# A row LSTM over a 128 x 128 image: the products of input channels 0-63 as three 64-row products per pixel pair, in pairs, with one PSUM ring and a written order

## The chip, the cores and the metric

One core of a Trainium2 chip. The metric is device time of one execution in microseconds (us); lower is better. Times are medians over the runs of one job unless a profile is named. A profile is of one execution.

Words used: a **half-step** is one image row for one half of the batch (4 of 8 images); there are 128 rows and two halves, so 256 half-steps. A **gate tile** is 128 of the 384 gate channels; there are three, A, B and C. A **unit** is one fp32 product with 128 rows of weights and 256 columns; by the records it is two **passes**. A **change of row tiling** is a switch of TensorE between products of 128 rows and products of 64 rows, which can lie two at a time in the array. In the lines of the profile, PE is TensorE's products, PEld its weight loads, DVE VectorE, ACT ScalarE, POOL GpSimd.

## The reference, cut to what matters

```python
# x: (8, 96, 128, 128) fp32; normalised over 32 groups of channels, then
its = conv(gn(x), W_is * mask, 1 x 3)            # taps: left neighbour and (masked) centre
def step(carry, row_in):                          # over the 128 rows
    h, c = carry
    gates = conv(h, W_ss, 3) + row_in             # taps: left, centre, right along the row
    f, i, o = sigmoid(...), sigmoid(...), sigmoid(...)
    g = tanh(...)
    c = f * c + i * g
    h = o * tanh(c)
    return (h, c), h
out = x + h of all rows
```

The rows depend on each other through h; the two batch halves do not, so the kernel alternates them.

## The kernel before

Pixels are held as even and odd ones. With the sum vs = e + o and the difference vf = o - e of neighbours, two products of 256 columns give the three-tap convolution's common part (m1 + m2 for even pixels, m1 - m2 for odd ones), and two more on the shifted differences vd finish it. The contraction has 128 rows: 96 channels of h, and below them channels 64 to 95 of x. Channels 0 to 63 of x cannot fit there. They have a tile xn of their own, 64 channels shifted by a pixel above the same 64 channels unshifted, and one 512-column product of 128 rows.

```python
    def normalise_own(engine, s, k, j, lo, hi):
        norm(engine, xn[s][k % 2][:, lo:hi, :, j, :],
             xr[s][:, j, lo * W : hi * W].rearrange("p (r j t) -> p r t j", r=hi - lo, t=2), 0, 1, s * BH + j)
    ...
        def both(self, a):
            self.mm(a, 0, 1, self.vs, start=True)
            self.mm(a, 1, 2, self.vf)
        def copy(self, a):
            ...
            nc.scalar.activation(
                self.m1[a], self.ps[a][:, 0:HB], AF.Identity, bias=bias[:, a : a + 1]
            )
        def sums(self, a):
            lo, hi = self.ps[a][:, 0:HB], self.ps[a][:, HB : 2 * HB]
            nc.vector.tensor_add(lo, self.m1[a], hi)
            nc.vector.tensor_sub(hi, self.m1[a], hi)
        def rest(self, a):
            xi = xn[self.s][self.row // R % 2][:, self.row % R]
            self.mm(a, None, 4, xi.rearrange("p t b j -> p (t b j)"))
            self.mm(a, 0, 0, self.vd[:, 1])
            self.mm(a, 1, 3, self.vd[:, 0], stop=True)
    ...
    for row in range(NT):
        for s in range(NH):
            ...
            now.both(a0); prev.tanh(a2); prev.gated(); now.copy(a0); now.sums(a0)    # joined here
            ...
            now.rest(a0); now.tanh(a0); now.sigmoid(a0)
            ...
```

PSUM has a pool of two banks for each gate tile, and two banks for the statistics.

## Time and profile before

| | before |
|---|---|
| median | 2143.21 us (2142.21 to 2143.75, 3 runs) |
| head, up to half-step 1 | 142 us, loads and group statistics |
| recurrence, 255 half-steps | 1990 us |
| TensorE busy in the recurrence | all of it |
| granted clock | 0.997 |

The busy line says how long each engine had work; the chain says what set the end. The two differ for an engine that is busy and not late. Here the same engine leads in both, and the lines that show it stand in the prediction below. Two lines are added from the waits of the kernel before; the columns are who waited for whom, then us in total, times, longest us:

```profile
POOL vd L327 <- DVE vf L326: 753.9, 202, 19.9
ACT g L380 <- PE ps L354: 469.5, 767, 2.1
```

GpSimd (POOL) waited 754 us for work. It has room. ScalarE waited for the products, as everyone does behind the engine that sets the pace.

### The profile page before, as it was taken

What the parts mean: (1) busy time and instruction counts of PE and PEld (TensorE: products, weight loads), DVE (VectorE), ACT (ScalarE), POOL (GpSimd) and SP (SyncE); (2) the same over time, 40 slices, a digit from 0 to 9 for tenths busy, and PEclk for the clock granted to TensorE, in tenths of its full rate; (3) what the DMA queues carried; (4) which work ended last, traced back from release to release, by engine and by line L of the source; (5) the groups of instructions that cost most, each with busy time, mean ns of one, the idle gap of its engine ahead of it and who ended that gap; (6) DMA issues with size and microseconds to landing.
All of it is one profiled execution on the core that took longest, in us unless ns stands there. A gap on an engine that the chain in (4) does not pass through costs nothing.

```text
span 2140.7 us, 24553 instructions
## 1 busy us (share of the span) xinstructions
PE 2014.5 (94%) x7738; PEld 1451.8 (68%) x7738; DVE 1571.4 (73%) x3268; ACT 1387.0 (65%) x2611; POOL 1037.4 (48%) x1365
## 2 busy tenths in 40 slices
PE   0079999999999999999999999999999999999998
PEld 0057777777777777777777777777777777777776
DVE  6887777777777777777777777777777777777776
ACT  2446666666666666666666666666666666666666
POOL 1126555555555554555555555555555555555542
PEclk9999999999999999999999999999999999999999
DMA  9984234444323444432344443234444323444411
GB/s 395 421 249 94 76 81 109 108 109 95 75 76 80 109 108 109 97 72 77 80 109 109 109 101 71 76 79 109 108 109 93 80 75 79 109 109 109 100 38 30
DMA packets 104303, 236.46 MB, mean 110 GB/s; under 512 B 6000, under 2 KB 10352, under 8 KB 98288
## 3 DMA queue, kind: packets, MB, share of 16 engines
q1 hardware_dynamic: 104176, 234.91, 42.9%
q8 instruction: 62, 1.02, 0.2%
q14 instruction: 65, 0.53, 0.1%
HBM read 184.55 MB, written 50.33 MB: 110 GB/s over the span
## 4 chain that ended last, share of the span: by engine, by line
PE 93%; DMA 4%; DVE 2%; ACT 0%; SPq 0%; issue 0%; POOL 0%; POOLq 0%; ACTq 0%
PE ps L354 93%; DMA piece<-in_x_dram 3%; DVE bst L528 2%; DMA xn<-in_x_dram 1%; PE spin L153 0%; ACT piece L184 0%; ACT piece L187 0%; SPq L517 0%; DVE st L534 0%; PE pv L221 0%; DVE ps L371 0%; ACT L184 0%; PE dm L221 0%; DVE ps L370 0%; DVE hx L409 0%
## 5 line engine op out<-in xcount | busy, mean ns | idle before, releaser
L354 PEld LDWEIGHTS ps<-vd,wl 128*128 128x128 f32 x3072 | 583.7, 190 | 407.1 <-issue 366.7
L354 PE MATMUL ps<-xn,wl 128*128 128x512 f32 x1536 | 795.6, 599 | 0.6 <-DVE ps L371 0.6
L354 PE MATMUL ps<-vd,wl 128*128 128x256 f32 x3072 | 788.4, 379 | 0.0
L380 ACT ACTIVATE g<-ps 32x512 f32<-32x512 f32 x768 | 453.5, 590 | 469.5 <-PE ps L354 469.5
L327 POOL TENSOR_TENSOR vd<-hx 128x512 f32<-128x512 f32 x256 | 266.0, 1039 | 946.5 <-DVE vf L326 753.9
L364 ACT ACTIVATE m<-ps,wl 128x256 f32<-128x256 f32 x768 | 358.2, 466 | 181.8 <-PE ps L354 181.8
L354 PE MATMUL ps<-vs,wm 128*128 128x256 f32 x1536 | 457.8, 380 | 0.0
L354 PE MATMUL ps<-vf,wm 128*128 128x256 f32 x1536 | 457.1, 379 | 0.0
L384 ACT ACTIVATE ps<-ps 96x512 f32<-96x512 f32 x768 | 442.9, 577 | 16.2
L388 DVE TENSOR_TENSOR ps<-ps,c 96x512 f32<-96x512 f32 x256 | 178.0, 695 | 372.7 <-ACT ps L384 372.7
L371 DVE TENSOR_TENSOR ps<-m,ps 128x256 f32<-128x256 f32 x768 | 329.2, 429 | 26.3
L370 DVE TENSOR_TENSOR ps<-m,ps 128x256 f32<-128x256 f32 x768 | 324.5, 422 | 16.9 <-ACT m L364 1.4
L416 POOL TENSOR_TENSOR x<-x,hx 96x512 f32<-96x512 f32 x254 | 328.4, 1293 | 0.0
L354 PEld LDWEIGHTS ps<-xn,wl 128*128 128x128 f32 x1536 | 270.5, 189 | 74.5 <-DVE ps L371 32.4
L354 PEld LDWEIGHTS ps<-vs,wm 128*128 128x128 f32 x1536 | 292.2, 190 | 40.1 <-DVE vs L325 0.2
L354 PEld LDWEIGHTS ps<-vf,wm 128*128 128x128 f32 x1536 | 292.3, 190 | 39.9
L391 DVE TENSOR_TENSOR g<-ps,g 96x512 f32<-96x512 f32 x256 | 175.9, 687 | 106.8 <-ACT g L380 106.8
L279 POOL TENSOR_SCALAR hx<-x,rstd,nmr 32x512 f32<-32x512 f32 (+2 forms) x256 | 206.2, 805 | 25.4
L279 POOL TENSOR_SCALAR xn<-xr,rstd,nmr 128x512 f32<-128x512 f32 (+2 forms) x256 | 207.2, 809 | 0.2
L409 DVE TENSOR_TENSOR hx<-ps,th 96x512 f32<-96x512 f32 x256 | 173.8, 679 | 0.7 <-ACT th L399 0.7
L395 DVE TENSOR_TENSOR c<-ps,g 96x512 f32<-96x512 f32 x256 | 173.8, 679 | 0.0
L399 ACT ACTIVATE th<-c 96x512 f32<-96x512 f32 x256 | 158.0, 617 | 2.1 <-DVE c L395 2.1
(80 smaller groups left out, 448.5 us busy)
## 6 DMA issues: line engine op xcount, KB each, us to landing
xr<-in_x_dram SPq DMA_DIRECT2D x124, 512.0 KB, 9.2
x<-in_x_dram SPq DMA_DIRECT2D x62, 768.0 KB, 8.9
out_dram<-x SPq DMA_DIRECT2D x62, 768.0 KB, 5.3
piece<-in_x_dram SPq DMA_DIRECT2D x16, 1024.0 KB, 11.7
x<-in_x_dram SPq DMA_DIRECT2D x62, 256.0 KB, 6.2
xs<-in_x_dram SPq DMA_DIRECT2D x15, 1024.0 KB, 12.3
xn<-in_x_dram SPq DMA_DIRECT2D x15, 1024.0 KB, 12.5
out_dram<-x SPq DMA_DIRECT2D x2, 576.0 KB, 3.7
```

The lines of the kernel that those rows point to most:

```text
L279: engine.tensor_scalar(dst, src, scale, shift, ALU.mult, ALU.add)
L327: diff = nc.gpsimd.tensor_sub(vd.rearrange("p t (b j) -> p t b j", b=BH), strided(h[:, 0, 0, :], 1, [(BH * JP - 1, 2), (JP, BH), (1, J)]), ...
L354: nc.tensor.matmul(o, wt[p][:, bass.ts(a, P)], rhs, start=start, stop=stop, skip_group_check=True)
L364: nc.scalar.activation(self.m1[a], self.ps[a][:, 0:HB], AF.Identity, bias=bias[:, a : a + 1])
L370: nc.vector.tensor_add(lo, self.m1[a], hi)
L371: nc.vector.tensor_sub(hi, self.m1[a], hi)
L380: nc.scalar.activation(self.g[a * 32 : (a + 1) * 32], self.ps[a][C:P], AF.Tanh)
L384: nc.scalar.activation(gate, gate, AF.Sigmoid)
L388: nc.vector.tensor_mul(f, f, cs[self.s].rearrange("p t b j -> p (t b j)"))
L391: nc.vector.tensor_mul(self.g, self.ps[1][0:C], self.g)
L395: nc.vector.tensor_add(c, self.ps[0][0:C], self.g)
L416: (nc.gpsimd if row + 1 < NT else nc.vector).tensor_add(xo, xo, h)
```

## The change

The intent is to give TensorE fewer columns. Channels 0 to 63 get the same sum-and-difference treatment as h: P on the sum of a pixel pair, Q on the difference e - o, and E on the difference between the previous odd pixel and this one. Each has 64 rows and 256 columns. The data and the weights are stored twice, in rows 0-63 and in rows 64-127, and gate tile A uses the low half, B the high one and C one or the other by batch half, so that two products can lie side by side in the array. Nine products of 64 rows in 4.5 pairs should cost 4.5 units where the three 512-column products cost six. In return GpSimd makes the pair sums and differences, one of three bias copies moves to VectorE, all PSUM tiles share one ring of eight banks, and one written order covers two half-steps, with P and Q issued a half-step ahead.

```diff
-        tc.tile_pool(name="ps", bufs=2, space=bass.MemoryType.PSUM)
+        tc.tile_pool(name="ps", bufs=8, space=bass.MemoryType.PSUM)
...
+    def combine(xw, n, total, differences):
+        e, o = xw[:, 0:n, 0:J], xw[:, 0:n, J + 1 :]
+        nc.gpsimd.tensor_add(total, e, o)
+        nc.gpsimd.tensor_sub(
+            differences,
+            strided(xw[:, 0, :], 0, [(W + 1, n), (J, 2), (1, J)]),
+            strided(xw[:, 0, :], J + 1, [(W + 1, n), (0, 2), (1, J)]),
+        )
+    def own_image(s, k, j):
+        to = xs[s][k % 2]
+        widen(nc.gpsimd, xw[0], 0, R, s, j, 0)
+        combine(xw[0], R, to[:, :, 0, j, :], to[:, :, 1:3, j, :])
...
+        def own(self, a, i):
+            low = a == order["A"] or (a == order["C"] and self.s == 0)
+            rhs = self.xs[:, i].rearrange("p b j -> p (b j)")
+            self.mm(a, i % 2, wo[i], rhs, slice(0, C2) if low else slice(C2, P))
...
         def copy(self, a):
...
+            if a == order["A"] and self.row + self.s > 0:
+                nc.vector.tensor_scalar(self.m1[a], m1, column, None, ALU.add)
+            else:
+                nc.scalar.activation(self.m1[a], m1, AF.Identity, bias=column)
...
-            self.mm(a, None, 4, xi.rearrange("p t b j -> p (t b j)"))
...
+    PERIOD = (
+        "2A 1A siB' fg' 2B taB' cpA 1B loA 3C' cpB hiA 0C' loB 1C taC' hiB 2C siC' 0A gt'",
+        "3A cpC ce' 0B loC th' hiC", "X", "ou' F' S' D' re'", "3B taA siA",
+    )
+    PRODUCTS = (
+        "P+A P+B Q+A Q+B P+C P*A Q+C EA EB EC",
+        "Q+A P+B P+C Q+B Q+C EB EA EC",
+    )
```

In the written order, a mark `'` is the half-step before, `+` the next one, `*` the one after that; 1, 2, 0, 3 are the products on vs, vf and the two of vd; "X" is replaced by the two lines of PRODUCTS in turn.

## The prediction

> **What bounds the kernel now.** I read the page from the top: busy shares, slices, the chain that ended last, then the groups, and last two stretches of the timeline. First the busy shares, the PE slices and the chain (part 1, part 2 and part 4 of the page of the kernel before):
>
> ```profile
> PE 2014.5 (94%) x7738; PEld 1451.8 (68%) x7738; DVE 1571.4 (73%) x3268; ACT 1387.0 (65%) x2611; POOL 1037.4 (48%) x1365
> PE   0079999999999999999999999999999999999998
> ...
> PE 93%; DMA 4%; DVE 2%; ACT 0%; SPq 0%; issue 0%; POOL 0%; POOLq 0%; ACTq 0%
> ```
>
> TensorE has work from the third slice to the end and 93% of the chain is its products. A busy PE need not be a fast PE, so I looked at the pitch. The chain in order of time has a single piece for the whole recurrence:
>
> ```profile
> 142.83 1990.10 PE ps L354 x7650
> ```
>
> That is 255 half-steps (128 rows, two batch halves, the first one done in the head): 1990.1 / 255 = 7.80 us each, and 7650 / 255 = 30 records, so each of the 15 fp32 products of a half-step is two passes. The timeline of TensorE alone, one half-step:
>
> ```profile
> 2109.39 0.59 PE L354 MATMUL ps<-vs,wm 128*128 128x256 f32 x2
> 2109.82 0.59 PE L354 MATMUL ps<-vf,wm 128*128 128x256 f32 x2
> ...
> 2111.98 1.05 PE L354 MATMUL ps<-xn,wl 128*128 128x512 f32 x2
> 2112.87 1.03 PE L354 MATMUL ps<-vd,wl 128*128 128x256 f32 x4
> ```
>
> A 256-column product starts 0.43 us after the one before it (2109.39 to 2109.82), the 512-column one takes twice that (0.89, 0.86 elsewhere), the two vd products 0.86 together. In units of 256 columns a half-step has 3 x (1 + 1 + 2 + 2) = 18, and 7.80 / 18 = 0.433 us a unit. The array is full, at a granted clock of 0.997; only fewer columns, or columns side by side, make this shorter. The head (142.8 us, mostly input loads) and the tail (some 7 us) are fixed costs.
>
> **What the Trainium skill says.**
> - "TensorEngine Tiling (Array Packing)", Key Properties: tiles run independently and in parallel, and changing the tiling mode drains the engine. Its gotcha on PSUM pressure says that row tiles must not be in one bank at once; the change sends the members of a pair to different banks. The kernel before has only 128-row products, so its trace shows none of this.
> - "TensorE: Matmul & The Clock Gate", LDWEIGHTS and Part 3: a weight load costs by its columns, not its rows, and products start and end in program order. The trace before agrees on order. On the loads it has a usable number: the 4-column products of the statistics, which are nearly all load.
>
> ```profile
> 135.68 0.36 PE L221 MATMUL dm<-st,wl 128*128 128x4 f32 x2 [4.28 <-DVE st L534]
> 135.90 0.59 PE L221 MATMUL pv<-st,wl 128*128 128x4 f32 x4
> ```
>
>   Two passes in 0.22 us: 0.11 us a load, although the record of one says 0.190 in the groups. Today a pass of 0.215 hides one load easily.
> - "SBUF — State Buffer", Who interferes with whom: a VectorE instruction with two SBUF inputs and a GpSimd instruction that reads SBUF block each other. The trace before is arranged to avoid it: GpSimd's vd waits for VectorE's vf for 753.9 us in all, and vs and vf take 428 and 418 ns.
>
> **The change part by part.** The groups that I price from:
>
> ```profile
> L384 ACT ACTIVATE ps<-ps 96x512 f32<-96x512 f32 x768 | 442.9, 577 | 16.2
> L388 DVE TENSOR_TENSOR ps<-ps,c 96x512 f32<-96x512 f32 x256 | 178.0, 695 | 372.7 <-ACT ps L384 372.7
> L371 DVE TENSOR_TENSOR ps<-m,ps 128x256 f32<-128x256 f32 x768 | 329.2, 429 | 26.3
> L416 POOL TENSOR_TENSOR x<-x,hx 96x512 f32<-96x512 f32 x254 | 328.4, 1293 | 0.0
> L327 POOL TENSOR_TENSOR vd<-hx 128x512 f32<-128x512 f32 x256 | 266.0, 1039 | 946.5 <-DVE vf L326 753.9
> ```
>
> *TensorE.* Removed: three 512-column 128-row products, 6 units, 2.60 us. Kept: 12 units, 5.20 us. Added: nine 64-row products of 256 columns (P, Q, E for three gate tiles). Alone each would still cost a unit; in pairs on the two row halves they cost 4.5 units = 1.95 us, so at best 7.15 us a half-step, 0.65 less. Three things stand against the 1.95. (1) Loads: a pair has four passes, so four loads; 4 x 0.11 = 0.44 against 0.433, about 2.00 for 4.5 pairs. (2) An fp32 product is two passes in program order, so the low product's second pass can run beside the high product's first: full rate inside a run, but one extra pass, 0.217, at the end of each of the run (one run per half-step). (3) Two mode changes per half-step. Two passes that start 0.215 apart end 0.59 after the first start, so a pass lives 0.375, 0.16 beyond its stream; if a drain exposes all of it, 2 x 0.16 = 0.32. Sum if all of it shows: 5.20 + 2.00 + 0.22 + 0.32 = 7.74 us. I take the middle of 7.15 and 7.74, because nothing in this trace says how much of (2) and (3) the hardware hides: **7.44 us**, 0.36 less than now.
>
> *VectorE.* One of three bias copies moves to it from ScalarE (about 0.43, estimated from the 128x256 row). Work: sums 3 x (0.429 + 0.422) = 2.55, the four 96x512 steps 0.695 + 0.687 + 0.679 + 0.679 = 2.74, vs and vf 0.85, copy 0.43: 6.57 us, up from 6.14. Fits in 7.44, but little is left.
>
> *ScalarE.* 2 copies x 0.466 + 3 x 0.590 + 3 x 0.577 + 0.617 = 5.05 us, down from 5.52. Not a bound.
>
> *GpSimd.* vd 1.04, residual 1.29, two normalisations 0.81 each as now (3.95), plus the pixel-pair sum (about 0.52, half of the 128x512 row) and the two differences (1.04): 5.5 us. It fits, but in the old order GpSimd was idle whenever vf and vs ran; now it ends only about 1 us before them.
>
> *PSUM and order.* The eight banks in one ring let the x products of the next half-step (P, Q) run before h is there, so they fill what would be a wait for h. By the written order C's last product ends 2.75 us into a half-step, then tanh 0.6, gated 0.7, cell 0.7, tanh 0.6, output 0.7, vf 0.4: about 6.5 to 7.0, just ahead of the next half-step. The recurrence is off the path, with slack of half a microsecond or less.
>
> *Head.* More weights, GpSimd pair work for the first rows in one lump: I allow +5 us. So 2143 + 5 - 255 x 0.36 = 2056, given as **2055 us**.
>
> **The rivals.**
> - *No overlap of row tiles* (or loads that serialize with the 0.190 us of their records): 9 units instead of 4.5, or 4 x 0.19 = 0.76 a pair. Then 5.20 + 3.4 to 3.9 = 8.6 to 9.1 us, 2350 to 2470 us. For it: nothing here has shown two products side by side. Against it: the 0.11 pitch of the loads, the skill's page, and a schedule written around pairs that would make no sense otherwise. I give it 5%.
> - *VectorE becomes the bound.* Loop: the first tile's vs product starts, siB ends some 0.4 later, then fg, copy and all the rest, 6.57 with a few waits, until vs of the next half-step: about 7.15 to 7.25 with handovers. That is a floor of about 2000 us even where TensorE pairs ideally; it would show as PE waiting for vs or vf.
> - *GpSimd collides with vf and vs.* Where a block has two shared normalisations in one half-step, GpSimd needs 6.3 us and its last instruction can still run when vf wants to start; a wait of up to 0.8 in a quarter of the half-steps, some 50 us at worst, partly absorbed.
> - *Drains eat the gain*: all of (1) to (3) exposed, 7.74 us and 2130 to 2140 us, the same time as now.
>
> **Range and chances.** Ideal pairs with VectorE's floor give 1995; all costs exposed give 2133. So 1990 to 2130 for 8 in 10. Faster by over 2% needs under 2100, a half-step under 7.61. The estimate sits 0.17 below that, and the drains must be nearly fully exposed to miss it: 0.75. Within 2%: 0.16, the exposed drains or a collision. Slower: 0.09, no overlap or a new wait of VectorE and GpSimd.
>
> **What the profile after would show.** Right: pairs of 64-row products starting close together at 0.43 to 0.45 us a pair, a gap of 0.1 to 0.2 us at each entry and exit of their run, PE still over 90% of the chain, half-step near 7.4, VectorE at 88%, GpSimd near 72%. Wrong: a pair at 0.76 or more (loads or no overlap); PE idle with vf, vs or a sum as releaser (VectorE or GpSimd bound); vs and vf well above 0.43 us (collision); a head longer by much more than 5 us; or gaps at the mode changes larger than 0.16.

## The result, and the profile after

The changed kernel took 2087.9 us (2086.93 to 2088.49, 4 runs) beside 2143.48 us for the kernel before on the same chip: a ratio of 0.9741, interval 0.9724 to 0.9758. A ratio is the mean time of one kernel's runs over that of the other's of the same rounds, so it is not quite the ratio of the medians. It is faster by 2.6%, inside the range, with a gain of 56 us where 88 were forecast.

The busy shares and the chain by engine, of the page of the changed kernel:

```profile
PE 1949.5 (93%) x10810; PEld 1586.3 (76%) x10810; DVE 1704.4 (82%) x3522; ACT 1322.2 (63%) x2352; POOL 1449.1 (69%) x1636
...
PE 91%; DMA 3%; POOL 2%; DVE 2%; ACT 1%; issue 0%; SPq 0%; POOLq 0%
```

TensorE still leads both. GpSimd rose from 48% to 69% and is new in the chain, with 2%. The chain in order of time says where that 2% lies (start us, us, what; the view shows the longest pieces alone, and these are the last five of them up to the long one):

```profile
204.75 7.64 PE ps L376 x40
213.35 1.04 POOL vd L476
214.40 1.25 POOL x L493
217.15 1.03 POOL xs L312
218.22 1855.35 PE ps L376 x10360
```

From 218 us to 2074 us the chain is TensorE alone: 10360 passes of 42 a half-step are 246.7 half-steps in 1855.35 us, 7.52 us each (7.80 before). Before that, GpSimd's work is threaded through the chain. These are two different stories, so the traces were compared at fixed marks, the starts of VectorE's vf of a half-step:

| mark | before | after | after minus before |
|---|---|---|---|
| vf of half-step 1 | 142.11 | 146.25 | +4.1 |
| vf of half-step 11 | 218.89 | 234.32 | +15.4 |
| vf of half-step 255 | 2122.79 | 2069.40 | -53.4 |
| end | 2140.7 | 2086.6 | -54.1 |
| mean half-step, 20 to 240 | 7.803 | 7.521 | -0.282 |

The steady part gains 244 x 0.282 = 68.8 us. The head and the first ten half-steps lose 15.4, where the steady pace would have given 2.8 in those ten. The rest of this section is the steady part: TensorE's timeline over one run of 64-row products.

```profile
999.43 0.59 PE L376 MATMUL ps<-vd,wl 128*128 128x256 f32 x2
999.95 1.57 PE L376 MATMUL ps<-xs,wx 64*128 64x256 f32 x12
1001.35 0.38 PE L376 MATMUL ps<-xs,wl 64*128 64x256 f32 x1
1001.36 0.38 PE L376 MATMUL ps<-xs,wx 64*128 64x256 f32 x1
1001.57 0.38 PE L376 MATMUL ps<-xs,wl 64*128 64x256 f32 x1
1001.58 0.38 PE L376 MATMUL ps<-xs,wx 64*128 64x256 f32 x1
1001.78 0.60 PE L376 MATMUL ps<-xs,wl 64*128 64x256 f32 x4
1002.31 0.70 PE L376 MATMUL ps<-vd,wl 128*128 128x256 f32 x2
```

The records at 1001.35 and 1001.36 are passes of two products, one on each row half; the next two follow 0.22 us later. The pairs run wholly side by side. Ten products, 20 passes, fill 999.95 to 1002.31, 2.36 us; 5 x 0.432 would be 2.16. The missing 0.2 is one half of what the two ends of the run cost; the other half falls on the 128-row passes beside it. Single records, over 225 runs between 300 and 2000 us, have these medians: a steady step between passes is 0.216; the last 128-row pass to the first 64-row pass is 0.309, and that one to the next of its row half 0.320; at the exit 0.306 and 0.320. So an entry costs 0.093 + 0.104 and an exit 0.090 + 0.104, **0.39 us a half-step**. The first pass behind each change is itself longer (0.70 for two records at 1002.31, 0.59 elsewhere). Then 16.5 units x 0.432 + 0.39 = 7.52, the measured half-step; the formula has nothing left over.

The groups that answer to those of before (line, engine, operation, out<-in, shapes, count | busy us, mean ns | idle before, releaser):

```profile
L476 POOL TENSOR_TENSOR vd<-hx 128x512 f32<-128x512 f32 x256 | 266.4, 1041 | 464.9 <-DVE vs L466 461.9
L376 PE MATMUL ps<-xs,wx 64*128 64x256 f32 x3072 | 457.7, 394 | 3.1 <-POOL xs L311 2.5
...
L376 PEld LDWEIGHTS ps<-xs,wx 64*128 64x128 f32 x3072 | 322.7, 187 | 112.1 <-issue 84.2
L436 DVE TENSOR_TENSOR ps<-ps,c 96x512 f32<-96x512 f32 x256 | 178.0, 695 | 267.5 <-ACT ps L432 267.5
...
L493 POOL TENSOR_TENSOR x<-x,hx 96x512 f32<-96x512 f32 x254 | 329.6, 1298 | 0.0
...
L312 POOL TENSOR_TENSOR xs<-xw 128x512 f32<-128x512 f32 x256 | 274.1, 1071 | 0.0
```

A weight load of 64 rows has a record as long as one of 128 (187 against 190 ns), yet two of them fit under one pass of 0.216. VectorE's idle time ahead of its forget step fell from 373 to 268 us, GpSimd's ahead of vd from 947 to 465: both are fuller, neither is late once the recurrence runs.

### The profile page after: what moved, and what is told of

Its sections match the earlier page's. It is cut to its first block, busy times and chain, and to the rows that moved or that the text cites. A ratio compares the mean times of both kernels' runs of the same rounds, so it can differ in the third digit from the quotient of the medians.

```text
span 2086.6 us, 31236 instructions
## 1 busy us (share of the span) xinstructions
PE 1949.5 (93%) x10810; PEld 1586.3 (76%) x10810; DVE 1704.4 (82%) x3522; ACT 1322.2 (63%) x2352; POOL 1449.1 (69%) x1636
## 4 chain that ended last, share of the span: by engine, by line
PE 91%; DMA 3%; POOL 2%; DVE 2%; ACT 1%; issue 0%; SPq 0%; POOLq 0%
PE ps L376 90%; DMA piece<-in_x_dram 2%; DVE bst L669 1%; DMA wl<-in_w_dram 1%; DMA xs<-in_x_dram 1%; PE spin L167 0%; POOL xw L295 0%; POOL hx L295 0%; POOL xs L312 0%; POOL vd L476 0%; POOL x L493 0%; ACT piece L200 0%; ACT piece L203 0%; SPq L658 0%; POOL xs L311 0%
## 5 line engine op out<-in xcount | busy, mean ns | idle before, releaser
L376 PE MATMUL ps<-vd,wl 128*128 128x256 f32 x3072 | 816.5, 388 | 5.0 <-POOL vd L476 4.3
L376 PE MATMUL ps<-xs,wx 64*128 64x256 f32 x3072 | 457.7, 394 | 3.1 <-POOL xs L311 2.5
L432 ACT ACTIVATE ps<-ps 96x512 f32<-96x512 f32 x768 | 418.8, 572 | 16.4 <-PE ps L376 0.2
L376 PEld LDWEIGHTS ps<-xs,wx 64*128 64x128 f32 x3072 | 322.7, 187 | 112.1 <-issue 84.2
L418 ACT ACTIVATE m<-ps,wl 128x256 f32<-128x256 f32 x513 | 243.5, 475 | 89.1 <-PE ps L376 75.4
L312 POOL TENSOR_TENSOR xs<-xw 128x512 f32<-128x512 f32 x256 | 274.1, 1071 | 0.0
L376 PE MATMUL ps<-xs,wl 64*128 64x256 f32 x1536 | 264.7, 376 | 1.5 <-DVE ps L425 1.3
L295 POOL TENSOR_SCALAR hx<-x,rstd,nmr 32x512 f32<-32x512 f32 (+1 forms) x260 | 206.6, 794 | 26.7
L295 POOL TENSOR_SCALAR xw<-xr,rstd,nmr 128x512 f32<-128x512 f32 (+1 forms) x264 | 210.8, 799 | 1.0
L376 PEld LDWEIGHTS ps<-xs,wl 64*128 64x128 f32 x1536 | 195.2, 187 | 20.3 <-DVE ps L425 3.0
```

Of the source, the lines that this page charges most:

```text
L295: engine.tensor_scalar(dst, src, scale, shift, ALU.mult, ALU.add)
L312: nc.gpsimd.tensor_sub(differences, strided(xw[:, 0, :], 0, [(W + 1, n), (J, 2), (1, J)]), strided(xw[:, 0, :], J + 1, [(W + 1, n), (0, 2) ...
L376: nc.tensor.matmul(self.ps[a][:, bass.ts(half, HB)], weights[rows, bass.ts(a, P)], rhs[rows], start=new, stop=False, skip_group_check=True,)
L418: nc.scalar.activation(self.m1[a], m1, AF.Identity, bias=column)
L432: nc.scalar.activation(gate, gate, AF.Sigmoid)
```

## The experiments

Theory, after reading both traces: (a) pairs of 64-row products overlap fully, (b) each change of row tiling costs 0.20 us that nothing hides, (c) TensorE alone sets the steady pace, and (d) GpSimd's work holds up the first ten half-steps (in the words of the text expected for e9: it has more work in them than they last). Twelve kernels ran.

| run | median us | ratio to before | half-step, 20 to 240 |
|---|---|---|---|
| before | 2143 | 1 | 7.803 |
| c0, the changed kernel | 2088.05 | 0.9742 | 7.521 |
| e1, runs split | 2189.22 | 1.0216 | 7.919 |
| e2, all on one row half | 2568.94 | 1.1988 | 9.457 |
| e3, as 128-row products | 2471.79 | 1.1534 | 9.065 |
| e4, less TensorE work | 1888.81 | 0.8814 | 6.699 |
| e5, same half adjacent | 2091.45 | 0.9760 | 7.528 |
| e6, copy back on ScalarE | 2098.01 | 0.9789 | 7.553 |
| e7, own rows on ScalarE | 2102.28 | 0.9811 | 7.521 |
| e8, as e7 and more | 2098.84 | 0.9794 | 7.521 |
| e9, shared rows on ScalarE | 2079.35 | 0.9705 | 7.521 |
| e10, head copies moved | 2086.69 | 0.9738 | 7.521 |
| e11, runs of nine and nine | 2141.30 | 0.9993 | 7.734 |

### e1: two runs of 64-row products in a half-step

```diff
         "2A 1A ... siC' 0A gt'",
+        "Y",                       # P+A P+B, or Q+A P+B: the first pair of X
         "3A cpC ce' 0B loC th' hiC", "X", ...
```

> The first pair of each run of 64-row products is written earlier, so that every half-step has two runs of 64-row products instead of one, with the same products. Theory (each change of the row tiling costs about 0.20 us that nothing hides, read from the trace: 0.093 us more between the two passes and 0.104 us more in the first pass after it): two more changes per half-step, 0.39 us, and 255 of them make +100 us: about 2188 us. Rival (the 0.39 us is a fixed cost of the products themselves, or other work hides it): 2085 to 2095 us.

Measured 2189.22 us, +101 on the changed kernel; the half-step grew by 0.398. The gaps at each change kept their lengths (0.309, 0.320, 0.306, 0.320), and there were twice as many. The cost is of the change of tiling, not of the products, and nothing hides it.

### e2 and e3: no pairs, and no change of tiling

```diff
-            self.mm(a, i % 2, wo[i], rhs, slice(0, C2) if low else slice(C2, P))
+            self.mm(a, i % 2, wo[i], rhs, slice(0, C2))     # e2
+            self.mm(a, i % 2, wo[i], rhs, slice(0, P))      # e3, with
+        nc.gpsimd.memset(wx[C2:P], 0.0)
+        nc.gpsimd.memset(tap[3][C2:P], 0.0)
```

> All 64-row products read rows 0 to 63 (the data and weights are the same in both row halves, so the result stays right). Theory (pairs run wholly side by side, 4.5 units of 0.432 us for nine products): nine units one after the other, +4.5 x 0.432 = 1.94 us a half-step, about 2088 + 255 x 1.94 = 2583 us. Rival (the pairs that the trace shows start together but share something, so they are worth less than half): clearly below 2500 us.

> The same nine products as 128-row products, the weights of rows 64 to 127 set to zero (result right): no change of tiling at all and no pairs. Theory (change of tiling costs 0.39 us a half-step): 0.39 x 255 = 100 us less than the kernel with all products on one side, about 2483 us. Rival (no cost in the change of tiling): the same time as that kernel, about 2583 us.

TensorE's timeline in e2, one run of 64-row products and its two ends:

```profile
1004.22 1.46 PE L376 MATMUL ps<-vd,wl 128*128 128x256 f32 x6
1005.61 2.42 PE L376 MATMUL ps<-xs,wx 64*128 64x256 f32 x10
1007.88 1.46 PE L376 MATMUL ps<-xs,wl 64*128 64x256 f32 x6
1009.26 0.70 PE L376 MATMUL ps<-vd,wl 128*128 128x256 f32 x2
```

Eight products take 3.65 us here and 1.93 in the changed kernel. A half-step of e2 is 9.457 us: 1.936 above 7.521, against 4.5 x 0.432 = 1.94. Each product takes a whole unit when it has no partner, so the pairs are worth all of their overlap. e3 has the same products without a change of tiling, and its half-step is 0.392 us shorter than that of e2 (9.065), 97 us in all. That is the second, independent measure of the 0.39. Both came out 11 to 14 us below the expected totals. Half-steps 1 to 11 took 94.3 us in e2, ten times 9.43, about its steady pace (9.457): a slower half-step leaves GpSimd time, and the loss of the first ten half-steps, which the expected totals had kept in, does not arise.

### e4: what would bound the kernel next (wrong result)

```diff
         def t_(self, a):
-            self.own(a, 2)
+            return
         def m0_(self, a):
-            self.mm(a, 0, wt[0], self.vd[:, 1])
+            return
```

> Wrong result on purpose: the E products and the first of the two vd products are left out, which takes three 128-row units and three 64-row products from a half-step: TensorE needs 9 x 0.432 + 3.5 x 0.432 + 0.39 = 5.8 us. Theory (TensorE is the only bound; VectorE's loop is the next, a floor of 7.15 to 7.25 us): half-step 7.15 to 7.25 us, 1995 to 2020 us, with TensorE waiting for vf, vs or sums. Rival (VectorE's loop already bounds the changed kernel): within 10 us of 2088. Rival (next bound far away): 1700 us.

1888.81 us and 6.70 us a half-step: TensorE was the bound, and VectorE is next, but at 6.70 rather than 7.15. The chain of e4 in order of time, one turn of the loop:

```profile
1008.17 0.44 DVE vf L471
1008.60 0.04 issue
1008.65 1.15 PE ps L376 x4
1009.79 0.03 issue
1009.82 0.49 DVE m L416
1010.34 0.44 DVE ps L421
...
1014.19 0.60 DVE hx L453
1014.81 0.44 DVE vf L471
```

The chain goes from vf through two products of TensorE (1.15 us) to the bias copy, so vs (0.43) and the forget step (0.70) run beside those products and are not in the loop. The turn of 6.64 us is 5.30 of VectorE's other instructions (as the chain counts them, without their overlap), 1.15 of products and 0.19 of handovers. The prediction had counted vs and the forget step in series. The expected 1995 to 2020 us was missed on this account.

### e5: order inside a run

```diff
-        "P+A P+B Q+A Q+B P+C P*A Q+C EA EB EC",
-        "Q+A P+B P+C Q+B Q+C EB EA EC",
+        "P+A Q+A P+B Q+B P+C P*A Q+C EA EB EC",
+        "Q+A P+C P+B Q+B Q+C EB EA EC",
```

> In each run of 64-row products two products of one row half are written next to each other, then two of the other (low low high high), otherwise as the changed kernel. Theory of the prediction (strict program order of passes): the second half waits for the first one's passes, some three passes of 0.216 us a half-step, about +150 us. Rival (each row half has its own order, and the engine looks ahead by at least one product): within 10 us of 2088.

The edit reorders the first four products of a run. 2091.45 us; the half-step grew by 0.007 us, not 0.6, and the runs by 0.007 (1.934 and 2.366 us). Two products of one half next to each other in the program do not keep the other half waiting, and in the changed kernel itself the first records of a run start 0.007 us apart. The prediction's extra pass from program order does not exist. Whether the engine looks ahead or the build places the two passes of a product otherwise cannot be told from these records.

### e11: a product without a partner

```diff
-        "P+A P+B Q+A Q+B P+C P*A Q+C EA EB EC",
-        "Q+A P+B P+C Q+B Q+C EB EA EC",
+        "P+A P+B Q+A Q+B P+C Q+C EA EB EC",
+        "P+A P+B Q+A Q+B P+C Q+C EB EA EC",
```

> The one product that is written two half-steps ahead (P of the first tile, every second half-step) is written one half-step ahead like the others, so that the runs have nine and nine 64-row products instead of ten and eight: five on one row half and four on the other in each. Theory (a product without a partner costs as much as a pair, 0.432 us): ten pair times in two half-steps instead of nine, +0.216 us a half-step, +55 us, about 2143 us, the time of the kernel before. Rival (the odd product overlaps with the change of tiling or with neighbours of the other run): 2088 to 2100 us.

2141.30 us, a ratio of 0.9993: the same work, and the whole gain is gone. The run of nine takes 2.356 us in the mean (median 2.353), as long as the run of ten (2.359): five products on one row half are ten passes, whether the other half has four or five. TensorE's timeline of e11, the end of a run:

```profile
1008.38 0.48 PE L376 MATMUL ps<-xs,wl 64*128 64x256 f32 x1
1008.59 0.38 PE L376 MATMUL ps<-xs,wx 64*128 64x256 f32 x1
1008.70 0.38 PE L376 MATMUL ps<-xs,wl 64*128 64x256 f32 x1
1008.81 0.38 PE L376 MATMUL ps<-xs,wx 64*128 64x256 f32 x1
1008.92 0.38 PE L376 MATMUL ps<-xs,wl 64*128 64x256 f32 x1
```

With a partner missing, the two halves run out of step (0.11 apart) and nothing is saved by it. The small change of the written order, one product two half-steps ahead, is worth as much as the whole change gains: 53 us of 55.

### c0: the changed kernel again

> The changed kernel itself, as the measure for the three beside it: 2088 us, 0.974 of the kernel before.

2088.05 us, ratio 0.9742 (0.9729 to 0.9755), as expected.

### e6: the bias copy back on ScalarE

```diff
-            if a == order["A"] and self.row + self.s > 0:
+            if False:
```

> The first gate tile's bias copy goes back from VectorE to ScalarE in every half-step. Theory (TensorE alone sets the pace; recurrence has 0.6 us of slack): the same time as the changed kernel within 3 us. Rival (VectorE is close enough to the bound that its 0.48 us matter): 10 us or more faster; or ScalarE's order makes sums later and it is slower.

2098.01 us, 10 us slower than c0. A miss of the theory as it was written. The first of the two lines is from the waits of e6, the second from those of the changed kernel:

```profile
DVE ps L421 <- ACT m L418: 236.1, 255, 4.2
```

```profile
DVE ps L421 <- ACT m L418: 0.2, 1, 0.2
```

The theory's second rival, later sums, is what came. With the copy on ScalarE, VectorE waits 236 us in all for it, the sums of tile A come later, and the block of 128-row products takes 5.421 us where it took 5.378 (medians; 0.032 on the mean half-step, 8 us of the 10). TensorE still leads the chain, with a small pause in it: within product 0 of tile A, by its place in the written order the first one added to the sums of that tile, the mean step between passes is 0.248 us, and 0.216 at the other steps of the block, the first one behind the exit apart. So the move to VectorE, which looks like a burden on the fuller engine, is part of the gain. ScalarE was busy for 714 of the 1000 us from 600 to 1600 with the copy and for 663 without it, so its total work was not the limit; its place in the order is the likely reason.

### e7, e8: taking work off GpSimd, first attempt

```diff
-        return ... + [(own_row, nc.gpsimd, xw[0], 1, r)]
+        return ... + [(own_row, nc.scalar, xw[0], 1, r)]
-        return [(own_image, s, 1, j) for j in images]
+        return [(own_image, s, 1, j, nc.scalar) for j in images]      # e8 also: late shared rows,
+        at(4, 0) + 9: lambda: first_rows(0, R),                       # and these copies one event later
```

> The normalisations that feed the pixel-pair work of the first ten half-steps (own rows and own images) go from GpSimd to ScalarE. Theory (GpSimd's lump of work makes TensorE wait in the first ten half-steps, about 14 us against the steady pace): 4 to 9 us less than the changed kernel, vf of the half-step 11 earlier by as much. Rival (the waits come from ScalarE and VectorE's order or from the loads): no gain, or a loss where ScalarE's gates are pushed back.

> As e7, and also the late shared rows on ScalarE, and the copies of the first rows behind the ScalarE statistics of image 4 instead of ahead of them. Theory: 8 to 14 us less than the changed kernel (first ten half-steps 6 to 11, head 2 to 3). Rival (ScalarE now becomes the one that is late): no better than e7.

2102.28 and 2098.84 us, slower than c0 by 14 and 11. Half-steps 1 to 11 took 101.7 us in e7 against 87.2 in c0. The waits of e7 say why:

```profile
ACT xw L293 <- POOL xs L312: 22.1, 4, 7.4
```

The normalised row goes through a buffer, xw, that GpSimd empties. ScalarE's next write to it waits for GpSimd, up to 7.4 us, and the tanh and sigmoid behind it in ScalarE's order wait too. The rival was right about these kernels; they say nothing about (d), because the edit put a new wait on the path. e8 is 3.4 us faster than e7; in the profiles its half-step 1 starts 3.2 us earlier.

### e9 and e10: second attempt

```diff
+    def early(s, *images):
+        return shared(s, 1, *images, engine=nc.scalar)
+        return shared(1, 0, *range(BH), rows=(r, r + 1), engine=nc.scalar) + ...      # late(r), e9 only
-        late(1) + own(0, 0), late(2) + shared(0, 1, 0), own(0, 1, 2), ...    # shared rows on GpSimd
+        late(1) + own(0, 0), late(2), own(0, 1, 2) + early(0, 0, 1), ...     # on ScalarE, e9 only
-        at(4, 0) + 8: lambda: (A.squares(nc.scalar), A.to_sbuf(), first_rows(0, R)),
+        at(4, 0) + 8: lambda: (A.squares(nc.scalar), A.to_sbuf()),           # e9 and e10
+        at(4, 0) + 9: lambda: first_rows(0, R),
```

> Only the normalisations of channels 64 to 95 of the first ten half-steps go from GpSimd to ScalarE (12.7 us by the durations of the changed kernel's profile; they need no buffer that GpSimd holds, unlike the own rows, which waited for it in e7), and the copies of the first rows are issued behind the ScalarE statistics of image 4. Theory (GpSimd has more work in the first ten half-steps than they last): the first ten half-steps lose 7 to 13 us less, and with the head 2076 to 2083 us. Rival (ScalarE's gates are pushed back as in e7): no faster than the kernel with the moved copies alone.

> Only the copies of the first rows are moved behind the ScalarE statistics of image 4. Theory (they hold back ScalarE's statistics, which hold a load buffer, on the head's chain): the half-step 1 starts about 3 us earlier, as in e8, and the time is 2085 us. Rival (the first ten half-steps are bound by GpSimd, which starts from loads and not from the head): 2088 us.

e9 took 2079.35 us, ratio 0.9705 (0.9691 to 0.9720), 8.7 us less than c0; vf of half-step 11 came at 225.55 us, not 234.46. In the stretch from 150 to 220 us of the two profiles, the busy times are (the changed kernel first, then e9; columns are us of the stretch, then busy us and instructions of PE, PEld, DVE, ACT and POOL, then granted clock, DMA share, GB/s):

```profile
150.00:220.00 70.00, 61.88 (x334) 47.48 (x332) 49.50 (x99) 36.03 (x66) 60.10 (x76) 0.98 0.34 76
```

```profile
150.00:220.00 70.00, 67.81 (x374) 52.58 (x371) 55.04 (x114) 54.76 (x97) 51.97 (x62) 1.00 0.46 101
```

GpSimd went from 60.1 to 52.0 us of 70, ScalarE from 36.0 to 54.8, and TensorE from 61.9 to 67.8. Half-steps 1 to 11 took 79.69 us, 87.24 in c0, and 87.22 in e10, which has the moved copies alone: GpSimd's work did hold up the first ten half-steps. That its work is more than they last was too strong: in the profile of the changed kernel GpSimd is busy for 73.8 us in them, and ten at the steady pace would last 75.2. e9 is still 4.5 us above that, for which no run gives the reason. It is the fastest kernel with a right result.

e10 is unclear. Its profile starts half-step 1 3.4 us earlier, but e9, with the same edit, only 1.4 earlier, and the median is 1.4 us below c0 with overlapping intervals (0.9723 to 0.9752 and 0.9729 to 0.9755), and the profiled execution, at 2085.12 us, was the fastest of its four. What makes the head some 4 us longer is not settled.

## Why the prediction was right or wrong

The direction, a gain of over 2% and the range were right; the gain was 56 us where 88 were forecast. By its own steps:

- *TensorE bounds, 7.80 us a half-step, 0.433 a unit.* Right: e4 lifts the bound by taking work from TensorE alone.
- *Pairs at 4.5 units.* Right: e2 loses 1.936 of the 1.94 us.
- *Term (1), the loads, +0.05.* Not there: four loads of a pair hide under its passes (a step inside a run is 0.216).
- *Term (2), the extra pass, +0.22.* Not there: e5.
- *Term (3), the drains, at most 0.32.* Under-sized: 0.39, all exposed (e1, e3); at 0.20 a change, the prediction's own sign of being wrong, gaps over 0.16, came. The estimate had only the 0.16 us that a pass lives beyond its stream; the first pass behind a change is also 0.104 us longer.
- *"I take the middle of 7.15 and 7.74".* This is the step that failed. Of the three terms between the ends, 0.59 us together, the drains were there in full, 0.39 where 0.32 was allowed, and the other two not at all. The middle came to 7.44 by halving three terms of which one was real; measured 7.52, and 255 x 0.08 is 20 us.
- *VectorE 6.57 us and a floor of 7.15 to 7.25.* The work was right (6.63 as a sum of durations; as these overlap, VectorE is busy for 83% of a half-step, not 88%); the floor was not: e4 reaches 6.70.
- *GpSimd collides with vf and vs.* Only up to half-step 12: seven of the 512 instructions took over 0.5 us (vs up to 1.29, usually 0.42); the means are 437 and 426 ns. The trace agrees with the blocking that the Trainium skill describes in "SBUF — State Buffer", Who interferes with whom: each of the seven began while a GpSimd instruction that reads SBUF was running and ended 0.28 or 0.29 us after one (vs at 180.69 to 181.98 us, GpSimd's xs at 180.43 to 181.69). The steady order keeps clear of it.
- *The head, +5 us.* It was 4 in the head; the first ten half-steps then took 11 us more than before, where the steady pace would have saved 3. The prediction did not count these 14 although it named GpSimd's lump. Together 18 for 5.
- *Unforeseen:* that the bias copy's move is itself worth 8 to 10 us (e6), and that without the even count of each run the whole gain is gone (e11).

Some 20 us of steady pace and 13 of the start account for the missing 32. Not isolated: the ring of eight banks and the rest of the written order, which cannot be taken out alone without rewriting the order. No run tells their worth.

## What to carry to other kernels

When small products are packed side by side, count pairs in each run, not products: a product without a partner costs a full slot, and each run pays for entry and exit whatever it holds, so few long runs with as many products on one row half as on the other win. When an upper and a lower estimate differ by separate yes-or-no terms, decide each term, because their average is a time that no mechanism gives. And before work is moved to an idle engine, look at what that engine will wait for and what stands behind it in its order: moving normalisations from GpSimd to ScalarE cost 14 us where they went through a shared buffer (e7), and took 7.5 us off the same ten half-steps where others that need no such buffer were moved (e9).

## What the Trainium skill lacked or had wrong

- "TensorEngine Tiling (Array Packing)", Key Properties, says that a change of tiling mode drains the engine, without a size. Here it is 0.20 us per change with fp32 products of 256 columns: 0.09 us more between the passes and 0.10 us more in the first pass behind (0.39 us for the two of a half-step, by the records, by e1 and by e3 against e2). Nor does it say that a product left without a partner in a run takes as long as a pair: a run of nine took 2.356 us, a run of ten 2.359.
- "TensorE: Matmul & The Clock Gate", Part 3, has products in strict program order of start. Between the two row halves this did not show as a limit on the time: with its first four products written low, low, high, high, a run took 1.934 us instead of 1.927, and its first two records still start 0.013 us apart, one on each half as it seems (the records do not name the half). One of its points also says that a weight load overlaps products in flight only where the row group differs, though the mechanism described above it in the same Part allows for a background weight buffer too. The point alone is too narrow here: in the kernel before, all products use all 128 rows, loads have records of 0.190 us, and the passes still follow each other by 0.216.
